# A Mamba and attention layer pair with two expert networks: the second layer's experts dealt out over seven more steps, their sums fetched by plain loads, the flags formed earlier

## The chip, the core and the metric

The kernel runs on one core of one Trainium2 chip. A core has TensorE (PE in the profile; PEld is its weight load), VectorE (DVE), ScalarE (ACT), GpSimd (POOL) and SyncE (SP), which share an on-chip memory, SBUF; TensorE writes to PSUM, and transfers run on sixteen DMA engines. Each engine works through its own instructions in order and waits at semaphores for the others. The metric is the device time of one execution in microseconds, lower is better. Everything is in float32.

## The reference

The input is 8 sequences of 512 tokens with 256 features. Layer 0 adds a two-directional state-space block and a top-1 expert network to it, layer 1 an attention and a top-2 expert network with fixed capacity:

```python
xn = _layernorm(x)
x = x + _L0_attn_ref(xn, ...) + _L0_ffn_ref(xn, ...)
xn = _layernorm(x)
x = x + _L1_attn_ref(xn, ...) + _L1_ffn_ref(xn, ...)
```

The change lies in layer 1. Its attention has 16 heads of width 16; its keys and values come through a latent of width 64, and its scores are scaled, clipped and multiplied by a decay that falls with the distance:

```python
latent_kv = (k + v) @ W_down_kv
scores = clip(einsum('bhqd,bhkd->bhqk', qh, kh) * scale) * decay
out = einsum('bhqk,bhkd->bhqd', softmax(clip(scores)), vh)
return out @ Wo
```

Its expert network sends each of the 4096 tokens to its two best of eight experts. The eighth is a no-op that returns the token weighted; each of the other seven takes its first 512 tokens:

```python
h = relu(einsum('ceh,ehi->cei', inputs, experts_inter))
out = einsum('cei,eih->ceh', h, experts_out) * in_w[..., None]
combined = zeros_like(x_flat).at[used_idx].add(out)
combined = combined + x_flat * (noop_w * noop_mask)[:, None]
```

## The kernel before

**Layer 1 as a loop of steps.** Layer 0 and the routing fill the time until about 1120 us. What the change touches is the loop behind it (`for n in range(N + 2)`, from L1778 on): 128 steps, one for each of 8 batches, 4 groups of 4 heads and 4 blocks of 128 keys, so 16 steps a batch. The order in which instructions are recorded is the order in which each engine works them off. In iteration n stand, in this order: the scores of step n (`scores`: TensorE L1562, then VectorE's product with the decay band and its maxima, L1565, and two small operations, L1570 and L1572); up to six loads of the next batch's q and k rows (`load_some`, L1452, on SP); one move of each chain in `chains`; for step n - 1 ScalarE's exponentials (L1575, L1579) with calls of `soon()` and `fill(1)` between them; the values of step n - 2 (TensorE L1587); the weights of step n - 1 (`weigh`, VectorE L1583), which the values of the next iteration need; then `fill` again.

**Experts between the steps.** `experts()` is a generator over seven experts in two halves of 256 rows each. A half gathers its rows with indirect transfers (L1365, GpSimd), transposes them (L1382), multiplies in eight units with the first weights (L1405, ScalarE's relu L1408) and in eight units with the second (L1418), scales the result (L1422) and adds it into the array `x1` in DRAM with an indirect transfer that accumulates (L1423, GpSimd). Weights are loaded on SP's queue (L1374, L1400). `fill()` draws units while `spent` is below `due()`, a straight line that reaches all of `WORK` at step `LAST = 118`. A unit that stops in the middle of a second product yields True; until its next move `half_done` holds the generator.

**The end of a batch's attention.** `divide(b, g, ...)` is a chain, one move in each iteration. Its group's values go to DRAM (`od`, L1665). For a pair of groups, one iteration later, SP loads them back turned (`oT`, L1675) with the sums of the weights (`sm`, L1676); one iteration after that VectorE takes the minimum into `low` (L1681) and the reciprocals (L1682), SP writes and reads these spread out (`rd` L1683, `rb` L1685), and two iterations later VectorE multiplies (L1688). `oT` is a tile with one buffer for all batches. After the second pair, `finish(b, oT)` comes in front of the list `urgent`: four pieces, each with TensorE's product with the output weights (`fin`, L1522), ScalarE's copy (L1524) and VectorE's sum into the batch's rows in SBUF (`x_sb`, L1526). `soon()` takes one piece of `urgent`, but none while `half_done` is set:

```python
def soon():
    while urgent and not half_done and not late_left:
        if next(urgent[0], "end") != "end":
            return
        urgent.pop(0)
```

**The last batch and the end.** Batch 7 goes another way: its first two groups are turned by TensorE in `first_heads` (L1479 to L1485), also pieces of `urgent`, its last two behind the loop in four `Ending` objects with the parts `out`, `divide`, `back` and `project` (L1498 to L1516). `combine()` adds the experts' sums to `x_sb`: GpSimd issues accumulating loads from `x1` (L1534) for the batches 7 and 0 to 5, then for 6 once its `finish` is through, and then seven stores of whole batches (L1543). Batch 7's rows are stored by `project`, four transfers on SP (L1516). Last, VectorE makes a flag from `peaks`, `vmax` and `low` (L1851 to L1856), TensorE sums it over the partitions (L1858), VectorE casts it (L1860), all five engines read it, and a branch would run an exact version (`exact`) if it were not zero.

Of the kernel before, what the change touches and what calls it, by code (L numbers as in the profile page):

```python
# [17 lines left out]
P = 128  # L18
B, S, DM = 8, 512, 256
NT = B * S  # L20
NTILE = NT // P
TPB = S // P
# [27 lines left out]
KEEP, MOST, LEAST, WIDE = 30.0, 70.0, 1e-8, 1e4  # L50
# [13 lines left out]
def tile_kernel(ctx: ExitStack, tc: tile.TileContext, t, out: bass.AP):  # L64
    nc = tc.nc
    V, A, G, T, Y = nc.vector, nc.scalar, nc.gpsimd, nc.tensor, nc.sync
# [46 lines left out]
    x1 = dram.tile([NT, DM], FP, name="x1", tag="x1")  # L113
# [7 lines left out]
    def rows_of(src, b):  # L121
        return src[b * S : (b + 1) * S, :].rearrange("(c p) d -> p c d", p=P)
# [188 lines left out]
    order = [*range(2, B), 0, 1]  # L311
# [59 lines left out]
    def bank(name, shape, tag="gen"):  # L371
        return mp.tile(shape, FP, name=name, tag=("e", "s")[tag] if isinstance(tag, int) else tag, bufs=2)
# [6 lines left out]
    def rows_in():  # L379
# [29 lines left out]
        for u, b0 in zip(us, order[::2]):  # L409
# [17 lines left out]
            for k, b in enumerate(both):  # L427
# [5 lines left out]
                for o in range(KC):  # L433
# [7 lines left out]
                    else:  # L441
                        A.copy(xTs[b][:, o, :], tp)
            turned.append((both, halves))
        finish(2)
        return xTs

    def step_sizes():

        big = r0b
        v, u, z, z2 = (row(n).rearrange("p (t e) -> p t e", e=2 * NH) for n in ("sp_v", "sp_u", "sp_z", "sp_z2"))  # L450
        V.tensor_tensor(v, proj[:, :, : 2 * NH], bc(dt_bias, 1, D3), ALU.add)
        A.activation(u, v, AF.Abs)
# [12 lines left out]
        V.tensor_scalar(v, v, 0.0, None, ALU.max)  # L465
        V.scalar_tensor_tensor(dt.rearrange(f2), acc.rearrange(f2), 2.0, v.rearrange(f2), ALU.mult, ALU.add)
        V.tensor_scalar(ea, ea, -1.0, None, ALU.mult)
        for d in range(2):
            of = slice(d * NH, (d + 1) * NH)
            V.tensor_tensor(da[:, d], dt[:, :, of], bc(ea[:, of], 1, [P, NTILE, NH]), ALU.mult)  # L470
        yield
# [95 lines left out]
    with ExitStack() as es:  # L567
        p1, p2, psum = m1, m2, mp
# [644 lines left out]
        with tc.manual_schedule(engines=ENGINES):  # L1213

            rows, rest, sizes = itertools.chain(route0(), blocks()), late(), step_sizes()
# [136 lines left out]
    x_sb = res.tile([P, NTILE, DM], FP, name="x_sb", tag="x_sb")  # L1352
    with tc.tile_pool(name="a1", bufs=1) as p1, tc.tile_pool(name="a2", bufs=2) as p2, tc.tile_pool(
        name="ap", bufs=1, space=PSUM
# [100 lines left out]
        def inputs_of(b):  # L1455
            rows, vd = kept[b]
            got = {"q": [], "k": [], "v": p2.tile([P, TPB, VW], FP, name="vt", tag="vt")}
            Y.dma_start(out=got["v"], in_=vd)
            for n in ("q", "k"):
                spread(rows[n], got[n], n)  # L1460
            return got
# [56 lines left out]
        def finish(b, oT):  # L1518
            for c in range(TPB):
                fp = bank("fin", [P, DM])  # L1520
                for j in range(KC):
                    T.matmul(fp, oT[:, j, c * P : (c + 1) * P], w_o[:, j, :], start=(j == 0), stop=(j == KC - 1))  # L1522
                fo = p2.tile([P, DM], FP, name="fo", tag="fo")
                A.copy(fo, fp)  # L1524
                xi = x_sb[:, b * TPB + c, :]
                V.scalar_tensor_tensor(xi, xi, noop[:, b * TPB + c : b * TPB + c + 1], fo, ALU.mult, ALU.add)  # L1526
                yield
            finished.add(b)

        def combine():  # L1530


            def add(b):
                G.dma_start(out=x_sb[:, b * TPB : (b + 1) * TPB, :], in_=rows_of(x1, b), accum_op=ALU.add)  # L1534

            for b in (B - 1, *range(B - 2)):
                add(b)
            yield
            while B - 2 not in finished:
                yield  # L1540
            add(B - 2)
            for b in range(B - 1):
                G.dma_start(out=rows_of(out, b), in_=x_sb[:, b * TPB : (b + 1) * TPB, :])  # L1543

        class Step:
            def __init__(self, b, g, c, inputs):
# [103 lines left out]
        def divide(b, g, op, od, rd, held):  # L1652
# [37 lines left out]
            if g == 3:  # L1690
                urgent.insert(0, finish(b, oT))

        with tc.manual_schedule(engines=ENGINES):
            rows, vd = kept[0]
            got = {"q": [], "k": [], "v": p2.tile([P, TPB, VW], FP, name="vt", tag="vt")}
# [7 lines left out]
            low = p1.tile([P, 32], FP, name="low", tag="low")  # L1703
# [2 lines left out]
            for one in shared:  # L1706
                G.memset(one, 0.0)
            vmax = p1.tile([P, B], FP, name="vmax", tag="vmax")
            finished = set()
            urgent, idle, chains = [], [], []  # L1710
            WORK = NE1 * 2 * (1 + FC + 2 * 4)
            LAST = 118
            spent = 0

            def due():

                return WORK * (n - ready - 2) / (LAST - ready - 2) if ready else 0

            rows, work, ready, e1, number1 = combine(), None, None, None, None
# [57 lines left out]
            tails = []  # L1777
            for n in range(N + 2):  # L1778

                if n < N:  # L1780
                    b, g, c = steps[n]
                    if (g, c) == (2, 0) and b + 1 < B:
                        got = inputs_of(b + 1)
# [32 lines left out]
                if m >= 0:  # L1816
# [4 lines left out]
                    if s.c == TPB - 1:  # L1821
                        if m == N - 1:
                            tails = [Ending(s.b, c, s_op, s.scratch[2]) for c in range(TPB)]
# [8 lines left out]
                    elif spent < due():  # L1832
                        fill()
                follow()
            while urgent:
                soon()
            for _ in rows:
                pass
            for part in ("out", "divide", "back", "project"):
                for one in tails:  # L1840
                    getattr(one, part)()
            while urgent or chains:
                soon()
                for chain in list(chains):
                    if next(chain, "end") == "end":
                        chains.remove(chain)
            for _ in rows:
                pass

            flag = p1.tile([P, 3], FP, name="flag", tag="flag")  # L1850
            V.tensor_reduce(flag[:, 0:1], peaks, AX.X, ALU.max)  # L1851
            V.tensor_reduce(flag[:, 2:3], vmax, AX.X, ALU.max)
            V.tensor_scalar(flag[:, 1:2], flag[:, 2:3], WIDE, None, ALU.is_gt)
            V.scalar_tensor_tensor(flag[:, 0:1], flag[:, 0:1], MOST, flag[:, 1:2], ALU.is_gt, ALU.add)
            V.tensor_reduce(flag[:, 2:3], low, AX.X, ALU.min)
            V.scalar_tensor_tensor(flag[:, 0:1], flag[:, 2:3], LEAST, flag[:, 0:1], ALU.is_lt, ALU.add)  # L1856
            fp = bank("flags", [1, 1])
            T.matmul(fp, flag[:, 0:1], ones[:, 0:1], start=True, stop=True)  # L1858
            bad = p1.tile([1, 1], I32, name="bad", tag="bad")
            V.tensor_copy(bad, fp)  # L1860
            outside = nc.values_load(bad[0:1, 0:1], engines=list(ENGINES), min_val=0, max_val=3 * P)
            with tc.If(outside > 0):
                exact()
# [74 lines left out]
```

## Time and profile before

| what | us |
|---|---|
| median of 3 runs | 1750.51 (1749.23 to 1751.92) |
| the profiled execution | 1758.05 |
| its span, first to last instruction | 1755.9 |
| TensorE busy | 1592.3 |
| VectorE busy | 1193.0 |
| ScalarE busy | 919.0 |
| GpSimd busy | 571.2 |
| first scores of the loop | 1120.3 |
| last values of the loop end | 1740.45 |

The profiled execution took 7.5 more than the median of the timed ones. Times inside it are given from the start of its span. A row of a timeline gives the start, the duration, the engine, the line, the operation, what it writes and reads, how many follow each other, and in brackets the engine's idle time before it and what ended that. SPq rows are transfers that SP issues; they are short, since the transfer itself runs on the DMA engines. A wait for several semaphores is put down to the one that came last in the records, so a transfer named there can be a neighbour of the one that was waited for. TensorE's granted clock is 1.00 at full and 0.50 at half speed.

### The profile page before, as it was taken

How to read it: one execution, taken by the hardware profiler on the slowest of the kernel's cores; microseconds unless marked ns; L12 is line 12 of the kernel's file. 1: busy time of each engine (PE TensorE's matmuls, PEld its weight loads, DVE VectorE, ACT ScalarE, POOL GpSimd, SP SyncE). 2: the span in 40 equal slices, each digit the busy share in tenths (PEclk: the TensorE clock that was granted, in tenths of full speed). 3: DMA queues.
4: the chain of work that ended last, by engine and by line, in shares of the span. 5: the costliest groups of instructions: out<-in, count | busy, mean ns of one | idle time of the engine just before them, and what ended most of it. 6: DMA issues, size and time to landing. Idle time of an engine off the chain costs nothing.

```text
span 1755.9 us, 25860 instructions
## 1 busy us (share of the span) xinstructions
PE 1592.3 (91%) x8736; PEld 952.7 (54%) x8736; DVE 1193.0 (68%) x3111; ACT 919.0 (52%) x2173; POOL 571.2 (33%) x519
## 2 busy tenths in 40 slices
PE   6556799989999999999789889879999999999997
PEld 6323466767677677767455456544444444444432
DVE  6567685575676755865777657476777767767574
ACT  4232345345454454454545533337777777767674
POOL 0041465565565565653522421001111111112030
PEclk9776799999999999999999899769999999999896
DMA  8010355455564464554454624423424333343245
GB/s 299 12 54 0 131 173 186 157 186 177 164 210 158 157 211 150 188 192 134 103 138 139 163 95 115 116 98 86 134 82 116 109 103 113 92 117 118 56 71 148
DMA packets 131789, 230.56 MB, mean 131 GB/s; under 512 B 20093, under 2 KB 93823, under 8 KB 120512
## 3 DMA queue, kind: packets, MB, share of 16 engines
q1 hardware_dynamic: 101952, 119.46, 22.2%
q0 software_dynamic: 28656, 108.69, 20.5%
q8 instruction: 73, 1.20, 0.3%
q10 hardware_dynamic: 1040, 0.66, 0.2%
q14 instruction: 68, 0.56, 0.1%
HBM read 176.23 MB, written 53.05 MB: 131 GB/s over the span
## 4 chain that ended last, share of the span: by engine, by line
PE 42%; DVE 6%; ACT 1%; SPq 1%; issue 1%; DMA 1%; POOL 0%; ACTq 0%; DVEq 0%
PE s_ps L1562 8%; PE o_ps L1587 7%; PE e_hp L1405 6%; PE e_yp L1418 6%; PE fin L1522 2%; PE qp L265 1%; PE pj L933 1%; PE tab L230 1%; PE op L1078 1%; DVE s L1565 1%; PE pp L762 1%; PE seg L1121 1%; PE sp L1189 1%; PE kp L274 1%; PE yd L1159 1%
## 5 line engine op out<-in xcount | busy, mean ns | idle before, releaser
L1565 DVE CUSTOM_DVE_ANT_0 s<-s_ps,band 128x512 f32<-128x512 f32 x512 | 323.0, 687 | 152.8 <-PE s_ps L1562 152.7
L1579 ACT ACTIVATE s<-s,ng 128x512 f32<-128x512 f32 x512 | 334.0, 710 | 0.0
L933 PE MATMUL pj<-xT,w_w_in 128*128 128x512 f32 x384 | 199.9, 647 | 10.1 <-DVE cv L946 6.2
L1423 POOL DMA_INDIRECT x<-e_yo,number x28 | 45.0, 1606 | 431.9 <-ACT e_yo L1422 230.0
L1562 PE MATMUL s_ps<-qT,kT 16*128 16x512 f32 x1024 | 167.7, 694 | 4.4 <-DMA kT<-kd 4.4
L946 DVE SCALAR_TENSOR_TENSOR cv<-pj,w_conv_w,cv 128x511 f32<-128x511 f32 (+2 forms) x192 | 143.2, 747 | 22.4 <-ACT cv L942 17.9
L1587 PE MATMUL o_ps<-s,wv 128*32 128x512 f32 x1024 | 150.0, 659 | 5.5 <-DVE wv L1583 4.7
L1105 POOL TENSOR_TENSOR au<-da,half 128x512 f32<-128x512 f32 x64 | 76.4, 1193 | 235.6 <-PE seg L1121 163.1
L639 PEld LDWEIGHTS h_ps<-xdT,w 128*128 128x128 f32 x1152 | 139.1, 194 | 20.8 <-issue 20.0
L639 PE MATMUL h_ps<-xdT,w 128*128 128x128 f32 x1152 | 142.1, 277 | 2.2 <-DMA w<-in_w_dram,w_idx 2.2
L663 PE MATMUL y_ps<-w,hT 128*128 128x256 f32 x576 | 138.7, 385 | 0.0
L1418 PE MATMUL e_yp<-e_w,e_hT 128*128 128x256 f32 x448 | 125.8, 405 | 0.0
L1418 PEld LDWEIGHTS e_yp<-e_w,e_hT 128*128 128x128 f32 x448 | 77.5, 191 | 88.2 <-issue 65.5
L663 PEld LDWEIGHTS y_ps<-w,hT 128*128 128x128 f32 x576 | 108.3, 193 | 30.0 <-issue 16.1
L1405 PE MATMUL e_hp<-e_xdT,e_w 128*128 128x256 f32 x448 | 123.3, 400 | 0.0
L1405 PEld LDWEIGHTS e_hp<-e_xdT,e_w 128*128 128x128 f32 x448 | 78.6, 190 | 76.8 <-ACT e_hT L1408 37.7
L933 PEld LDWEIGHTS pj<-xT,w_w_in 128*128 128x128 f32 x384 | 70.4, 201 | 91.6 <-issue 81.9
L1134 ACT ACTIVATE mt<-seg,mid 64x64 f32<-64x64 f32 x512 | 109.4, 309 | 0.8
L1168 DVE TENSOR_TENSOR yT<-yT,yd 128x512 f32<-128x512 f32 (+1 forms) x64 | 43.8, 684 | 96.5 <-PE yd L1159 96.5
L950 ACT ACTIVATE th<-cv 128x512 f32<-128x512 f32 x64 | 40.3, 630 | 118.5 <-DVE cv L946 109.0
L942 ACT ACTIVATE cv<-pj,w_conv_b,w_conv_w 128x512 f32<-128x512 f32 x64 | 49.8, 778 | 89.9 <-PE pj L933 85.8
L1153 DVE TENSOR_TENSOR mt<-mt,cbm 128x1024 f32<-128x1024 f32 x64 | 94.1, 1471 | 1.2 <-ACT mt L1134 1.1
(339 smaller groups left out, 2794.6 us busy)
## 6 DMA issues: line engine op xcount, KB each, us to landing
ex<-exd SPq DMA_DIRECT2D x96, 128.0 KB
fr<-fdd SPq DMA_DIRECT2D x64, 128.0 KB
od<-os SPq DMA_DIRECT2D x28, 256.0 KB
e_w<-in_ei_dram SPq DMA_DIRECT2D x7, 1024.0 KB
e_w<-in_eo_dram SPq DMA_DIRECT2D x7, 1024.0 KB
vd<-vt SPq DMA_DIRECT2D x16, 272.0 KB
vt<-vd SPq DMA_DIRECT2D x8, 544.0 KB
u<-in_u_dram SPq DMA_DIRECT2D x8, 512.0 KB
```

The costliest lines, as they stand in the source:

```text
L639: T.matmul(hp[:, i, :], w1[:, k * FF + f * P : k * FF + (f + 1) * P], xdT[:, k * P : (k + 1) * P], start=(k == 0), stop=(k == KC - 1),)
L663: T.matmul(yp, hT[f // 4][:, f % 4, :], w2[:, f * DM : (f + 1) * DM], start=(f == 0), stop=(f == FC - 1),)
L933: T.matmul(pj, w_in[:, k, o * P : (o + 1) * P], self.xT[:, k, :], start=(k == 0), stop=(k == KC - 1))
L946: V.scalar_tensor_tensor(cv[:, s:], pj[:, : S - s], conv_w[:, q, 3 - s : 4 - s], cv[:, s:], ALU.mult, ALU.add)
L1134: A.activation(mt[lo, over, h], seg[lo, over, h], AF.Exp, bias=mid[lo, self.i, h : h + 1])
L1153: V.tensor_tensor(self.mt, self.mt, bc(self.cbm, 1, H3), ALU.mult)
L1405: T.matmul(hp, w1[:, k, f * P : (f + 1) * P], xdT[:, k, :], start=(k == 0), stop=(k == KC - 1))
L1418: T.matmul(yp, hT[:, f, c * P : (c + 1) * P], w2[:, f, :], start=(f == 0), stop=(f == FC - 1))
L1562: T.matmul(sp[i], self.k[r, cols], self.q[r, :], start=True, stop=True)
L1565: V.tensor_tensor_reduce(out=self.p[i], in0=sp[i], in1=band[:, at : at + S], scale=1.0, scalar=KEEP, op0=ALU.mult, op1=ALU.max, accum_out= ...
L1579: A.activation(self.p[i], self.p[i], AF.Exp, bias=self.ng[:, i : i + 1])
L1587: T.matmul(op[32 * i : 32 * i + 32, :], self.wv[:, i, :], self.p[i], start=(self.c == 0), stop=(self.c == TPB - 1),)
```

## The change

Four things change. `LAST` goes from 118 to 125, so that `due()` spreads the experts' units over seven more steps. `combine()` no longer accumulates by transfers: when the units are spent, the expert pools are closed, eight tiles `xa` take their place, SP loads `x1` into them with plain transfers, GpSimd adds the batches 7 and 0 to 4 and stores 0 to 4, and VectorE adds 5 and 6 after the loop, which GpSimd stores. The calls that emptied `urgent` and `rows` ahead of the last tiles' parts go. The flag's operations are recorded between these parts, with a fourth column for the minimum and the cast on ScalarE, and TensorE's sum stands ahead of `project`.

```diff
         def combine():
-            def add(b):
-                G.dma_start(out=x_sb[:, b * TPB : (b + 1) * TPB, :], in_=rows_of(x1, b), accum_op=ALU.add)
-
-            for b in (B - 1, *range(B - 2)):
-                add(b)
-            yield
-            while B - 2 not in finished:
+            es.close()
+            p3 = es.enter_context(tc.tile_pool(name="f3", bufs=1, side="right"))
+            order = (B - 1, *range(B - 1))
+            got = {}
+            for b in order:
+                got[b] = p3.tile([P, TPB, DM], FP, name="xa", tag=f"xa{b}")
+                Y.dma_start(out=got[b], in_=rows_of(x1, b))
+
+            def add(engine, b):
+                own = x_sb[:, b * TPB : (b + 1) * TPB, :]
+                engine.tensor_tensor(own, own, got[b], ALU.add)
+                if b < B - 1:
+                    G.dma_start(out=rows_of(out, b), in_=own)
+
+            for b in order[:-2]:
+                add(G, b)
+            while not closing:
                 yield
-            add(B - 2)
-            for b in range(B - 1):
-                G.dma_start(out=rows_of(out, b), in_=x_sb[:, b * TPB : (b + 1) * TPB, :])
+            for b in order[-2:]:
+                add(V, b)
+                yield
...
-            LAST = 118
+            LAST = 125
...
-            while urgent:
-                soon()
-            for _ in rows:
-                pass
-            for part in ("out", "divide", "back", "project"):
-                for one in tails:
-                    getattr(one, part)()
             while urgent or chains:
                 soon()
                 for chain in list(chains):
                     if next(chain, "end") == "end":
                         chains.remove(chain)
-            for _ in rows:
-                pass
-
-            flag = p1.tile([P, 3], FP, name="flag", tag="flag")
+            closing = True
+            flag = p1.tile([P, 4], FP, name="flag", tag="flag")
             V.tensor_reduce(flag[:, 0:1], peaks, AX.X, ALU.max)
             V.tensor_reduce(flag[:, 2:3], vmax, AX.X, ALU.max)
             V.tensor_scalar(flag[:, 1:2], flag[:, 2:3], WIDE, None, ALU.is_gt)
             V.scalar_tensor_tensor(flag[:, 0:1], flag[:, 0:1], MOST, flag[:, 1:2], ALU.is_gt, ALU.add)
-            V.tensor_reduce(flag[:, 2:3], low, AX.X, ALU.min)
-            V.scalar_tensor_tensor(flag[:, 0:1], flag[:, 2:3], LEAST, flag[:, 0:1], ALU.is_lt, ALU.add)
+            for part in ("out", "divide"):
+                for one in tails:
+                    getattr(one, part)()
+            V.tensor_reduce(flag[:, 3:4], low, AX.X, ALU.min)
+            V.scalar_tensor_tensor(flag[:, 0:1], flag[:, 3:4], LEAST, flag[:, 0:1], ALU.is_lt, ALU.add)
+            for one in tails:
+                one.back()
+            next(rows, None)
             fp = bank("flags", [1, 1])
             T.matmul(fp, flag[:, 0:1], ones[:, 0:1], start=True, stop=True)
             bad = p1.tile([1, 1], I32, name="bad", tag="bad")
-            V.tensor_copy(bad, fp)
+            A.copy(bad, fp)
+            for one in tails:
+                one.project()
+            for _ in rows:
+                pass
```

More of the change, by code (lines that the diff above doesn't have):

```diff
@@ L1527, in finish @@
                 yield
-            finished.add(b)
         def combine():
-            def add(b):
-                G.dma_start(out=x_sb[:, b * TPB : (b + 1) * TPB, :], in_=rows_of(x1, b), accum_op=ALU.add)
-            for b in (B - 1, *range(B - 2)):
-                add(b)
-            yield
-            while B - 2 not in finished:
+            es.close()
[13 more added lines that the diff above has]
+            while not closing:
                 yield
-            add(B - 2)
-            for b in range(B - 1):
-                G.dma_start(out=rows_of(out, b), in_=x_sb[:, b * TPB : (b + 1) * TPB, :])
+            for b in order[-2:]:
+                add(V, b)
+                yield
         class Step:
@@ L1708, in tile_kernel @@
             vmax = p1.tile([P, B], FP, name="vmax", tag="vmax")
-            finished = set()
+            closing = False
             urgent, idle, chains = [], [], []
             WORK = NE1 * 2 * (1 + FC + 2 * 4)
-            LAST = 118
+            LAST = 125
             spent = 0
```

## The prediction

> **What bounds the kernel now.** I read the page first, then the stretches of the last stage by window, then the chain of waits and the engines' timelines around the two places where TensorE stops, last the end.
>
> ```profile
> span 1755.9 us, 25860 instructions
> PE 1592.3 (91%) x8736; PEld 952.7 (54%) x8736; DVE 1193.0 (68%) x3111; ACT 919.0 (52%) x2173; POOL 571.2 (33%) x519
> ```
>
> ```profile
> 1600.00:1637.50 37.50, 37.50 (x212) 18.17 (x211) 27.08 (x98) 27.24 (x57) 5.35 (x4) 1.00 0.40 123
> 1637.50:1644.50 7.00, 5.04 (x28) 2.23 (x27) 2.37 (x11) 4.26 (x8) 0.00 (x0) 0.97 0.25 69
> 1644.50:1655.00 10.50, 10.01 (x36) 3.73 (x36) 6.67 (x25) 4.59 (x10) 1.63 (x1) 0.53 0.34 66
> 1655.00:1695.00 40.00, 40.00 (x230) 17.76 (x230) 29.48 (x108) 29.08 (x60) 3.60 (x3) 1.00 0.15 34
> 1708.00:1740.00 32.00, 28.76 (x118) 7.46 (x114) 19.28 (x76) 18.71 (x38) 6.76 (x9) 0.52 0.89 208
> ```
>
> Above the page, below it stretches of the last stage. Columns: stretch, length, busy time of PE, PEld, DVE, ACT, POOL, then the granted clock. While expert work is dealt out, PE is busy all the time at clock 1.00: the 128 attention steps go at PE's pace. Behind step 118 PE runs at 0.52. In between lies one hole, 1637.5 to 1655, with the clock at 0.53 after it.
>
> The price of a step is read from the chain of waits: scores 1.07, expert unit 1.06, values 0.99, expert unit 1.06, together 4.19; a further unit behind another adds 1.92 - 1.06 = 0.86.
>
> ```profile
> 1656.24 1.06 PE e_yp L1418 x4
> 1657.30 0.99 PE o_ps L1587 x8
> 1658.30 1.06 PE e_yp L1418 x4
> 1659.36 1.07 PE s_ps L1562 x8
> ...
> 1666.67 1.92 PE e_hp L1405 x8
> ```
>
> The hole, as timelines of SP's queue, VectorE and PE:
>
> ```profile
> 1629.53 0.34 SPq L1665 DMA_DIRECT2D od<-os  x1
> 1637.52 0.55 SPq L1675 DMA_DIRECT2D oT<-od  x1
> ...
> 1639.09 0.16 DVE L1572 TENSOR_SCALAR w<-peaks 128x4 f32<-128x4 f32 x1
> 1643.82 0.19 DVE L1681 TENSOR_TENSOR low<-low,sm 128x32 f32<-128x32 f32 x1 [4.57 <-DMA kT<-kd]
> ...
> 1636.36 1.13 PE L1522 MATMUL fin<-w_w_o,oT 128*128 128x256 f32 x4
> 1641.41 1.13 PE L1418 MATMUL e_yp<-e_w,e_hT 128*128 128x256 f32 x4
> 1644.99 1.94 PE L1587 MATMUL o_ps<-s,wv 128*32 128x512 f32 x8 [2.45 <-DVE wv L1583]
> ```
>
> `oT` has one buffer. SP cannot load batch 6's `oT` until PE has done batch 5's last `fin`: that ends at 1637.49, the load goes at 1637.52. Behind it stands the load of `sm`; VectorE, in order, waits for it in `low` (L1681) until 1643.82, 6.3 after `fin`; behind `low` stands `wv` (L1583), behind `wv` PE's values at 1644.99, 7.5 after `fin`. Count a batch's steps from its first: `low` stands in step 11 and holds the weights for the values that PE issues in step 12. In the built order the last `fin` of batches 0 to 5 stands in steps 10, 10, 10, 10, 11, 11 of the batch behind. At 10 the trace shows no hole; at 11 both batches have one: 2.23 of PE's idle time at 1570 (clock kept), and 2.45 at 1645, with the clock lost for some 10 us.
>
> **The change, part by part** (against the profiled run: span 1755.9, 1758.05 around it, 7.5 above the median of the timed runs; I carry the difference over to the median).
>
> *Experts to step 125.* 224 units in steps 8 to 118 become 224 in steps 8 to 125. The built order has 222 units done by the end of step 117 before and 208 after: 14 x 0.86 = 12.0 earlier. Steps 118 to 125: four with a `fin` and two units 5.05 each, one with two transposes 4.5, three at 4.19, together 37.3; before, scores of 118 to scores of 126 took 1727.2 - 1689.5 = 37.7. Sum: -12.4. Filling the cold steps with units costs them nothing, since without them they run at half clock.
>
> *What the new pace does to `fin`.* `soon()` does nothing while a y-part of an expert is half done, so another phase of the units moves the `fin`s. In the changed order the last one of batches 0 to 5 stands in steps 11, 12, 12, 12, 10, 9. At 12, PE reaches the values held up right behind it: `fin`, one unit (0.86), then values that may start 7.5 after `fin` (8.2 in the earlier hole): a hole of 6.6 to 7.4, I take 7.0. To that comes the clock: around the hole at 1645 two steps (scores to scores, 1640.34, 1648.86, 1655.1) took 8.52 and 6.24 where their parts sum to 4.19 and 3.72, so 6.85 more, of which 2.5 is the wait and 4.3 the half clock. The earlier hole of 2.2 cost 2.3. A hole of 7.0 is nearer to the one that lost its clock, being longer than both: 7.0 + 4.3 = 11.3 each, three times, 33.9; bounds 6.6 without and 7.4 + 5.0 where half of some 10 us at half clock is lost. Batch 1's hole (step 11) is of the old kind: 2.3 to 6.85, taken as 5.0. The two old holes go: -9.2. Sum: +29.7. `sm`, `rd`, `rb` and the next batch's kT loads move with SP; kT is needed four steps on and stays hidden.
>
> The row on the clock is 0.53 for 1644.5 to 1655 though PE was busy for 10.01 of the 10.50. The Trainium skill ("TensorE: Matmul & The Clock Gate", section "What's actually happening") has the array warm again after one busy window of about 3.4 us, at half rate until then. By that a lost clock would cost at most 1.7 in place of 4.3, and the sum would fall by some 9; this trace's row disagrees, and I keep the row.
>
> *First heads later.* Step 126 takes transposes and column work that stood in step 122: 5.0 there, 4.29 for a bare step at half clock: +1. From the scores of 127 to the last values 8.9 before; after, two more transposes but a warmer clock: 0, between -1 and +2.
>
> *Plain loads, adds, stores.* Now this:
>
> ```profile
> 1694.52 1.55 POOL L1423 DMA_INDIRECT x<-e_yo,number  x1 [6.83 <-ACT w L1575]
> 1698.90 10.53 POOL L1534 DMA_DIRECT2D x_sb<-x  x8 [2.83 <-DVE wv L1583]
> ...
> 1724.66 0.75 POOL L1543 DMA_DIRECT2D out_dram<-x_sb  x1 [1.91 <-DMA x_sb<-x]
> ...
> 1747.40 0.42 DVE L1515 TENSOR_TENSOR x_sb<-x_sb,finq 128x256 f32<-128x256 f32 x1 [0.44 <-PE finq L1514]
> ...
> 1749.44 0.15 DVE L1860 CAST bad<-flags 1x1 int32<-1x1 f32 x1 [0.28 <-PE flags L1858]
> ```
>
> The accumulating loads and the stores ended under the last steps; after step 118 they had 50 us. Now they have step 126 to the end. Let O be the end of the last values (1740.45 before). The scores of step 126 start at O - 14.1 (5.2 + 8.9). The last scatter lands 4.6 after the unit before them (1693.7 to 1698.3), the first 512 KB load needs some 2.9 (two such loads issued at 1604.9 were in at 1610.5, so 2.8 each): POOL starts adding at O - 6.6. No row has a 128x1024 add on POOL; 128x512 takes 1042 ns at the median in L1148 and 1260 in L1183, whose operands are alike: 2.1 to 2.5, taken 2.25. Six adds 13.5, seven stores issued at 0.75 to 0.96, 6.2: POOL is through at O + 13.1. VectorE meanwhile: `finq` adds end at O + 7.4 before; the low flag (0.34) and one 128x1024 add (1219 ns at the median in L1153) stand ahead of them, one behind: O + 10. POOL is later and sets the end. From the last `bad` read (1749.7) to the end there were 6.2; before, O + 15.4, now O + 19.3: +3.9, between +2.5 (adds of 2.1) and +6. The flag chain that leaves VectorE (1.6) lies before POOL's end and brings nothing.
>
> A pair of VectorE and POOL operations with two inputs in SBUF is the place where the Trainium skill ("SBUF — State Buffer", section "Who interferes with whom") speaks against the change: one waits for the whole other. L1153's longest, 6398 ns against a median of 1219, agrees with it. By the rule VectorE's two adds wait up to 2.25 each, O + 14.5; by the row's median O + 10; the end would move by 1.4 at most.
>
> **Sum:** -12.4 + 29.7 + 1 + 3.9 = +22.2: 1778 as a span, 1750.5 + 22.2 = **1772.7** as a median.
>
> **The rivals.**
> (a) *The late `fin` is hidden and no hole appears*: then -12.4 - 9.2 + 1 + 3.9 = -16.7, 1733.8. It decides if `sm` lands before VectorE is through with step 11, that is if the last `fin` is at least 6.3 ahead of `low`. For it: four batches show no hole now. Against: those have it in step 10, none in 12. Chance 0.09.
> (b) *Holes, but the clock holds*, as at 1570: 3 x 7.0 + 2.9 = 23.9 in place of 38.9: +7.2, 1757.7. Against: the longer of the two holes lost it. Chance 0.2.
> (c) *POOL becomes the bound by more*: adds twice as long as the row (L1105 has a longest of 2106 against 1042): 6 x 2.25 = +13.5, 1786. For it: VectorE works beside it; against: its scores read one operand from PSUM, and 1191 is the mean in L1020. Chance 0.1.
> The forecast itself has 0.61.
>
> **How the numbers follow.** The measurement tells about 0.2%, 3.5 us, from no change. Faster: (a) 0.09 and the low end of (b) 0.01. Same: 0.04 out of (b), where the holes are 6.6 and the tail +2.5. Slower: the rest, 0.86. The range runs from (b) less 3 to the forecast with holes of 12.5 (3 x 1.2) and batch 1 and the tail at their upper ends (2 + 2), with 5 more for (c): 1755 to 1785. Left out: (a) and most of (c).
>
> **What would show it.** `fin` before `oT` in SP's queue, and VectorE idle some 10 before `low` in batches 2, 3, 4 (steps 43, 59, 75), some 5 in batch 1; PE idle 6.6 to 7.4 at each of the three with the clock near 0.5 behind; no hole in batches 5 and 6. Units until step 125 at clock 1.00. At the end POOL adding after VectorE's `finq` adds. I am wrong if PE is busy without a break from step 10 to 125, or if POOL's adds end before the last values.

## The result and the profile after

The changed kernel takes 1773.99 us (median; 1771.48 to 1779.96), the kernel before 1749.87 (1739.02 to 1751.92) on the same chip: a ratio of 1.0137, with a 95% interval of 1.0100 to 1.0175. It is slower, by about as much as forecast (1772.7). Not every term of that sum was right, though, and two errors offset each other in part.

The profiled executions differ by less than the medians: spans of 1755.9 before and 1769.7 after, +13.8 against +24.1, because the one of before lay 8.2 above its median and the one of after 2.5 below its own. Executions of one kernel scatter here by some 0.5 to 0.8% to either side. The terms below are read from the two traces, the verdicts from the timed runs.

From the page of the kernel after, the span, the busy times, and the group of the values (out and in tiles, count, busy time, mean ns, then TensorE's idle time ahead of it and what ended most of that):

```profile
span 1769.7 us, 25893 instructions
PE 1585.9 (90%) x8736; PEld 948.5 (54%) x8736; DVE 1196.8 (68%) x3112; ACT 920.8 (52%) x2174; POOL 578.8 (33%) x517
...
L1593 PE MATMUL o_ps<-s,wv 128*32 128x512 f32 x1024 | 147.0, 649 | 21.1 <-DVE wv L1589 21.1
```

TensorE works 6.4 us less than before, and yet the span is 13.8 longer. It stands 21.1 us in front of the values, waiting for `wv`; the same group had 4.7 before.

The stage by window, around the hole in step 44 (stretch, length, busy time of PE, PEld, DVE, ACT, POOL, granted clock, share of the DMA engines, GB/s):

```profile
1300.00:1347.70 47.70, 47.70 (x276) 21.79 (x268) 34.98 (x126) 36.31 (x75) 9.17 (x7) 1.00 0.37 105
1347.70:1354.20 6.50, 3.08 (x17) 1.75 (x16) 0.00 (x0) 3.67 (x8) 0.00 (x0) 1.00 0.20 55
1354.20:1361.00 6.80, 3.26 (x11) 1.38 (x12) 4.20 (x16) 0.00 (x0) 0.00 (x0) 0.50 0.59 174
1361.00:1400.00 39.00, 39.00 (x228) 16.80 (x227) 28.75 (x104) 30.89 (x64) 5.36 (x4) 1.00 0.33 100
```

TensorE is busy without a break before and behind. Between 1347.7 and 1361.0 it stands for 6.95, and the clock is at 0.50 for 6.8, the first half of which falls into the standstill. VectorE does nothing at all in the first of the two stretches.

The same hole in the timelines of SP's queue, VectorE and TensorE (start, duration, engine, line, operation, tiles; in brackets the idle time before and what ended it):

```profile
1337.38 0.34 SPq L1671 DMA_DIRECT2D od<-os  x1
...
1339.62 1.03 SPq L1452 DMA_DIRECT2D kT<-kd  x2
1349.95 0.54 SPq L1681 DMA_DIRECT2D oT<-od  x1
1350.54 0.52 SPq L1682 DMA_DIRECT2D sm<-od  x1
...
1346.47 0.17 DVE L1578 TENSOR_SCALAR w<-peaks 128x4 f32<-128x4 f32 x1
1356.66 0.19 DVE L1687 TENSOR_TENSOR low<-low,sm 128x32 f32<-128x32 f32 x1 [10.03 <-DMA sm<-od]
...
1357.46 0.23 DVE L1589 TENSOR_TENSOR wv<-vt,w 128x68 f32<-128x68 f32 x1
...
1348.79 1.13 PE L1522 MATMUL fin<-w_w_o,oT 128*128 128x256 f32 x4
1349.76 1.03 PE L1405 MATMUL e_hp<-e_xdT,e_w 128*128 128x256 f32 x4
1357.74 1.94 PE L1593 MATMUL o_ps<-s,wv 128*32 128x512 f32 x8 [6.95 <-DVE wv L1589]
```

The heads of the pair were sent to DRAM at 1337, and from 1340.7 on nothing stands ahead of the load in SP's queue (with two `oT`, below, SP issues it right behind the same kT loads). Here it goes at 1349.95, right behind the old batch's last `fin` (1348.79 + 1.13). From there everything follows in a row: `sm` is in at 1356.6, VectorE has been idle for 10.03 in front of `low`, `wv` comes behind it, and TensorE's values 7.8 after `fin`, with one unit between. Steps 60 and 76 have the same picture with 6.08 and 6.15 of TensorE's idle time, step 28 the smaller one with 1.92.

The end of the kernel after, timelines of SP's queue, GpSimd, VectorE and TensorE (last values end at 1747.0):

```profile
1736.17 8.48 SPq L1537 DMA_DIRECT2D xa<-x  x8
...
1741.38 4.67 POOL L1541 TENSOR_TENSOR x_sb<-x_sb,xa 128x1024 f32<-128x1024 f32 x2 [7.67 <-DMA xa<-x]
...
1757.65 2.36 POOL L1541 TENSOR_TENSOR x_sb<-x_sb,xa 128x1024 f32<-128x1024 f32 x1
1760.32 2.26 POOL L1543 DMA_DIRECT2D out_dram<-x_sb  x3 [0.30 <-POOL x_sb L1541]
...
1750.23 2.90 DVE L1856 SCALAR_TENSOR_TENSOR flag<-flag 128x1 f32<-128x1 f32 x1
...
1758.75 0.42 DVE L1515 TENSOR_TENSOR x_sb<-x_sb,finq 128x256 f32<-128x256 f32 x1 [0.44 <-PE finq L1514]
...
1753.18 0.19 PE L1861 MATMUL flags<-ones,flag 128*1 128x1 f32 x2 [2.63 <-DVE flag L1856]
```

GpSimd adds from 1741.4 to 1760.0 and issues its last store until 1762.6, after VectorE's last `finq` sum (1759.2): GpSimd and its stores end the kernel, 22.7 behind the last values, against 15.4 before. A flag operation on one element per partition takes 2.90 in place of 0.16; TensorE waits 2.63 for it.

To set the traces side by side I counted for each step from 8 on what it takes beyond the parts of its work (the 4.19 with two units and the 0.86 of a third in the prediction):

| | before | after | difference |
|---|---|---|---|
| scores of step 8 start | 1187.2 | 1183.4 | -3.8 |
| steps 8 to 125 by their parts | 526.4 | 513.6 | -12.8 |
| beyond the parts (the holes) | 13.6 | 34.3 | +20.7 |
| scores of step 126 to the end of the last values | 13.25 | 15.7 | +2.45 |
| from there to the end | 15.45 | 22.7 | +7.25 |
| span | 1755.9 | 1769.7 | +13.8 |

(For before, the row of parts has 492.9 up to step 118 and 33.5 for the stretch from the scores of 119 to those of 126.) Of the 34.3, steps 28 and 29 hold 5.2, step 44 8.6, step 60 8.0 and step 76 8.0; of the 13.6, steps 92, 108 and 109 hold 9.15. Step 8 has some 3 in every run.

### The profile page after: what moved, and what is told of

Read it like the earlier page. It is cut to its first block, busy times and chain, and to the rows that moved or that the text cites. A ratio compares the mean times of both kernels' runs of the same rounds, so it can differ in the third digit from the quotient of the medians.

```text
span 1769.7 us, 25893 instructions
## 1 busy us (share of the span) xinstructions
PE 1585.9 (90%) x8736; PEld 948.5 (54%) x8736; DVE 1196.8 (68%) x3112; ACT 920.8 (52%) x2174; POOL 578.8 (33%) x517
## 3 DMA queue, kind: packets, MB, share of 16 engines
q1 hardware_dynamic: 106176, 123.66, 22.3%
## 4 chain that ended last, share of the span: by engine, by line
PE 43%; DVE 5%; DMA 1%; ACT 1%; SPq 1%; issue 1%; POOL 0%; DVEq 0%; ACTq 0%; POOLq 0%
PE s_ps L1568 8%; PE o_ps L1593 8%; PE e_yp L1418 7%; PE e_hp L1405 6%; PE pj L933 2%; PE fin L1522 2%; PE qp L265 1%; PE tab L230 1%; PE op L1078 1%; PE pp L762 1%; DMA sm<-od 1%; PE yd L1159 1%; PE seg L1121 1%; PE sp L1189 1%; PE kp L274 1%
## 5 line engine op out<-in xcount | busy, mean ns | idle before, releaser
L1593 PE MATMUL o_ps<-s,wv 128*32 128x512 f32 x1024 | 147.0, 649 | 21.1 <-DVE wv L1589 21.1
L1568 PE MATMUL s_ps<-qT,kT 16*128 16x512 f32 x1024 | 160.2, 678 | 4.6 <-DMA kT<-kd 4.6
L639 PEld LDWEIGHTS h_ps<-xdT,w 128*128 128x128 f32 x1152 | 137.7, 192 | 21.2 <-issue 20.4
L1405 PE MATMUL e_hp<-e_xdT,e_w 128*128 128x256 f32 x448 | 128.4, 411 | 0.0
L663 PEld LDWEIGHTS y_ps<-w,hT 128*128 128x128 f32 x576 | 106.8, 190 | 29.4 <-issue 16.1
```

The source lines that it names most:

```text
L639: T.matmul(hp[:, i, :], w1[:, k * FF + f * P : k * FF + (f + 1) * P], xdT[:, k * P : (k + 1) * P], start=(k == 0), stop=(k == KC - 1),)
L663: T.matmul(yp, hT[f // 4][:, f % 4, :], w2[:, f * DM : (f + 1) * DM], start=(f == 0), stop=(f == FC - 1),)
L1405: T.matmul(hp, w1[:, k, f * P : (f + 1) * P], xdT[:, k, :], start=(k == 0), stop=(k == KC - 1))
L1568: T.matmul(sp[i], self.k[r, cols], self.q[r, :], start=True, stop=True)
L1593: T.matmul(op[32 * i : 32 * i + 32, :], self.wv[:, i, :], self.p[i], start=(self.c == 0), stop=(self.c == TPB - 1),)
```

## The experiments

**Is the hole made by `oT`'s one buffer, and by the new pace alone?** My theory was that SP's `oT` load waits for the late `fin`. A rival was that the traffic of the units or the order of VectorE's work makes the holes in any case, another that the change of the end has a part in them. Four kernels tell these apart: a second buffer for `oT` in the kernel after and in the kernel before, `LAST` alone at 125 in the kernel before, and `LAST` back at 118 in the kernel after.

```diff
-                    held.append(p1.tile([P, KC, S], FP, name="oT", tag="oT"))
+                    held.append(p1.tile([P, KC, S], FP, name="oT", tag="oT", bufs=2))
```

(the same at the other two places that make an `oT`)

> The changed kernel with two buffers for oT, nothing else. Theory (the late fin holds SP's load of oT, that holds VectorE at low, that holds PE's values): the holes of steps 28, 44, 60, 76, together 31 us over the parts' sum in the changed kernel's trace, go, down to 1 or 2; time 1774 - 30 = 1744, 1739 to 1750. Rival A (the holes come from the experts' pace itself, by their weights' transfers on SP's queue): two buffers change nothing, 1774. Rival B (the change is slow by its end: GpSimd's adds and stores behind the last values): 1774 too, with the holes gone but the time not.

Measured: 1743.33 (1731.87 to 1748.68) against 1756.84 for the kernel before, a ratio of 0.9921 (0.9892 to 0.9951). The span of its profile is 1746.1. The time beyond the parts falls from 34.3 to 4.1, as expected; what is left lies mostly in step 8, and no step from 9 on has a hole. The end stays, at 23.1 behind the last values. Its timelines at the same batch:

```profile
1342.29 0.54 SPq L1681 DMA_DIRECT2D oT<-od  x1
1342.88 0.52 SPq L1682 DMA_DIRECT2D sm<-od  x1
...
1350.15 0.19 DVE L1687 TENSOR_TENSOR low<-low,sm 128x32 f32<-128x32 f32 x1 [1.78 <-DMA sm<-od]
...
1350.53 1.13 PE L1522 MATMUL fin<-w_w_o,oT 128*128 128x256 f32 x4
...
1352.46 1.06 PE L1593 MATMUL o_ps<-s,wv 128*32 128x512 f32 x8
```

The last `fin` is still late, at 1350.53, but SP has issued the loads 8.2 before it, `low` waits 1.78, and the values run on at full clock.

> The kernel before with two buffers for oT, nothing else. Theory: its two holes, 9.2 us with the half clock behind them, go: 1750 - 9 = 1741, 1737 to 1746. Rivals A and B: no difference, 1750.

Measured: 1751.90, a ratio of 0.9975 (0.9948 to 1.0002). Its profile has no hole either (4.2 beyond the parts in place of 13.6). In the traces that is worth 9.4; the timed runs show about 4.4, with an interval that just reaches no change. I had expected 9. So the two holes of the kernel before are real, but either they cost less in its usual execution than in the profiled one, or a second buffer costs something elsewhere; the runs don't settle which. With the second buffer on both sides the change is worth about 0.5% by the timed runs (0.9921 / 0.9975); the two profiled spans, 1746.1 and 1745.2, do not show it.

```diff
-            LAST = 118
+            LAST = 125
```

> The kernel before with the experts dealt out to step 125, and nothing else of the change. Theory: the order's fins stand as in the changed kernel, so the same four holes (31 us in place of 11, +20), the loop's units earlier (-12.5), and the accumulating loads and stores, 21 and 10 us of transfers in the trace of before, now start behind step 126 and end some 38 after its scores in place of 28.7: +9 to +11. 1750 + 20 - 12.5 + 10 = 1767, 1760 to 1774. Rival B (the end of the change alone is slow): no holes' cost, 1750 - 12.5 + 10 = 1748.

Measured: 1786.38, a ratio of 1.0176 (1.0120 to 1.0232). The kernel before with the new pace alone shows the holes of the kernel after, step by step: 5.4 in steps 28 and 29, 8.3, 8.4 and 7.9 in steps 44, 60 and 76, together 34.6 beyond the parts. So the pace makes them, without any part of the new end. Its timelines, TensorE in step 44 and GpSimd at the end:

```profile
1361.01 1.94 PE L1587 MATMUL o_ps<-s,wv 128*32 128x512 f32 x8 [6.60 <-DVE wv L1583]
...
1736.06 1.55 POOL L1423 DMA_INDIRECT x<-e_yo,number  x1 [6.83 <-ACT w L1575]
1740.56 10.53 POOL L1534 DMA_DIRECT2D x_sb<-x  x8 [2.96 <-DMA x<-e_yo,number]
...
1769.62 0.75 POOL L1543 DMA_DIRECT2D out_dram<-x_sb  x1 [4.26 <-DMA x_sb<-x]
```

The accumulating transfers, which were hidden at `LAST` 118, come out into the open: the end is 29.6 behind the last values. That is why it is slower than the 1% I had expected. Against it, the plain loads and adds of the change are worth 29.6 - 22.7 = 6.9 at this pace.

> The changed kernel with the experts dealt out to step 118 as before: plain loads, adds and the flags' new places stay. Theory: fins and holes as in the kernel before, and the adds lie under steps 120 to 127; from the last values to the end 15.4 less the flag chain's 1.6 plus one add of 1.2 and a store's issue: 1750, 1745 to 1755. Rival B: the adds cost where they stand, 1757 or more.

Measured: 1764.11 (1749.29 to 1774.47), a ratio of 1.0034 (1.0001 to 1.0067). I had expected no difference; the rival, that the adds cost where they stand, fits better. The end is as short as before (16.1), what lies beyond the parts is close to before (16.3 for 13.6), but the stretch from the scores of 119 to those of 126 takes 40.7 in place of 33.5. GpSimd, VectorE and TensorE in that stretch:

```profile
1720.76 2.36 POOL L1541 TENSOR_TENSOR x_sb<-x_sb,xa 128x1024 f32<-128x1024 f32 x1
1723.42 0.77 POOL L1543 DMA_DIRECT2D out_dram<-x_sb  x1 [0.30 <-POOL x_sb L1541]
1724.21 2.37 POOL L1541 TENSOR_TENSOR x_sb<-x_sb,xa 128x1024 f32<-128x1024 f32 x1
...
1720.59 2.56 DVE L1576 TENSOR_SCALAR ng<-peaks 128x4 f32<-128x4 f32 x1
...
1723.65 3.02 DVE L1589 TENSOR_TENSOR wv<-vt,w 128x68 f32<-128x68 f32 x1
...
1712.83 1.94 PE L1593 MATMUL o_ps<-s,wv 128*32 128x512 f32 x8 [3.33 <-DVE wv L1589]
...
1723.88 0.45 PE L1484 MATMUL tb<-ident,oq 128*128 128x128 f32 x1 [3.17 <-DVE oq L1470]
```

`ng` (0.17 elsewhere) ends at 1723.15 and GpSimd's add at 1723.12; `wv` (0.22 elsewhere) ends at 1726.67 and the next add at 1726.58. VectorE's small operations last until GpSimd's sum is through, and TensorE waits 3.33, 1.21 and 3.17 in these steps. `wv` is recorded from 1723.65 on, 0.56 ahead of its sum, while GpSimd still issues a store; the store is not what holds it, since under a store with no sum behind it `wv` took 0.21 (at 1725.90 in the last kernel below, with `LAST` at 122). The next kernel tests the sums as a cause: the same sums, in about the same steps, on VectorE.

```diff
-            for b in order[:-2]:
-                add(G, b)
+            for _ in range(4):
+                yield
+            for b in order[:-2]:
+                add(V, b)
+                for _ in range(3):
+                    yield
```

> In the kernel after with LAST at 118 the scores of step 119 to those of step 126 take 40.7 us, against 33.5 in the kernel before, and TensorE waits 3.33 and 1.21 and 3.17 there behind VectorE. Here the same six sums are added by VectorE in place of GpSimd, one behind the weights of each of the steps 119 to 124. My theory: an add on GpSimd (2.36 us) holds off VectorE's operations with two inputs in SBUF and the small ones of four columns until it ends, since 1.94, 2.40, 1.02, 2.56 and 3.02 us of such operations each end together with an add. Without adds on GpSimd no weights (wv) and no ng take over 0.3 in these steps; VectorE has some 4.2 us of work in a step with its own add (1.22), about what TensorE has at half clock, so the stretch from 119 to 126 falls to 33.5 to 35.5. The end stays at 15.5 to 16.5 behind the last values. The time falls from 1.0034 of before to 0.999 to 1.001. Rival: the eight plain loads, or the lost clock, hold TensorE up whichever engine adds; then the stretch stays at 39 or more and the time at 1.003 or above.

Measured: 1753.79 against 1754.97, a ratio of 1.0000 (0.9971 to 1.0029). The stretch is back to 34.5, as expected, and the end is 15.1 behind the last values (15.5 to 16.5 expected). The durations of `wv`, least, median and longest in ns, with GpSimd's sums (first fence) and with VectorE's (second):

```profile
L1589 DVE TENSOR_TENSOR wv<-vt,w x128: 165/223/3025, 1130.3 to 1748.9; 128x68 f32<-128x68 f32 x128
```

```profile
L1593 DVE TENSOR_TENSOR wv<-vt,w x128: 166/223/244, 1128.8 to 1739.1; 128x68 f32<-128x68 f32 x128
```

The longest falls from 3025 to 244. The eight plain loads are the same in both, and the half clock lies over both stretches, so it is GpSimd's sums that held VectorE off. The rival falls.

**Does it have to be the buffer?** If the cause is that the load stands behind a late `fin`, an earlier `fin` must do as well, with one buffer. So `soon()` may work while a second product is half done:

```diff
-                while urgent and not half_done and not late_left:
+                while urgent and not late_left:
```

> The changed kernel with one buffer for oT, but soon() no longer waits while a y-part is half done; the order then has the last fin in step 9 for every batch. Theory (the hole is the lateness of fin, and fin is late for half_done): no holes, steps 8 to 125 within 5 us of their parts' sum as with two buffers, against 34 in the changed kernel; time as with two buffers, 0.99 of the kernel before, 0.985 to 0.996. Rival (the second buffer helped in another way, by its place in memory or by letting oT load early): holes stay, 1.014.

Measured: 1744.32, a ratio of 0.9935 (0.9903 to 0.9967) to the kernel before (1753.38 here). The last `fin` stands in step 9 in every batch, and 6.7 remains beyond the parts; of the holes, 1.31 us of idle time is left in step 44, at full clock. In step 44 SP issues the `oT` load at 1343.68 with one buffer. What VectorE waited for in front of `low` (us, times), first in the kernel after, then in this one:

```profile
  DMA sm<-od: 26.4, 7
  DMA kT<-kd: 8.6, 1
```

```profile
  DMA sm<-od: 10.7, 8
```

Two edits that share nothing but that `fin` no longer stands before the load both take the long holes away. The rivals fall.

**What sets the end?** Starting from the kernel with two `oT`, the flag's two operations with two inputs in SBUF become operations with one, and TensorE's sum runs over three columns:

```diff
-            V.scalar_tensor_tensor(flag[:, 0:1], flag[:, 0:1], MOST, flag[:, 1:2], ALU.is_gt, ALU.add)
+            V.tensor_scalar(flag[:, 0:1], flag[:, 0:1], MOST, None, ALU.is_gt)
...
-            V.scalar_tensor_tensor(flag[:, 0:1], flag[:, 3:4], LEAST, flag[:, 0:1], ALU.is_lt, ALU.add)
+            V.tensor_scalar(flag[:, 2:3], flag[:, 3:4], LEAST, None, ALU.is_lt)
...
-            T.matmul(fp, flag[:, 0:1], ones[:, 0:1], start=True, stop=True)
+            for k in range(3):
+                T.matmul(fp, flag[:, k : k + 1], ones[:, 0:1], start=(k == 0), stop=(k == 2))
```

> The changed kernel with two oT buffers, and the flag's two operations with two SBUF inputs replaced by ones with one input, TensorE summing three columns. Theory on the end: a VectorE operation with two SBUF inputs waits for a GpSimd add (1.37 and 2.90 us for operations of 0.16); with one input it does not, so these take 0.16 and TensorE's flags wait 2.6 less; but GpSimd's adds and stores are through last and set the end: last values to end 23.1 becomes 22 to 23. Rival (the flags set the end): 20 to 20.5.

Measured: 1740.87 in a single execution, span 1739.2, and 22.9 from the last values to the end against 23.1 without the edit. VectorE's timeline:

```profile
1719.54 0.15 DVE L1856 TENSOR_SCALAR flag<-flag 128x1 f32<-128x1 f32 x1
1720.36 4.00 DVE L1541 TENSOR_TENSOR x_sb<-x_sb,xa 128x1024 f32<-128x1024 f32 x1 [0.67 <-DMA xa<-x]
1724.29 1.40 DVE L1515 TENSOR_TENSOR x_sb<-x_sb,finq 128x256 f32<-128x256 f32 x4
```

The flag takes 0.15 now, under one of GpSimd's sums, and TensorE's flag sum no longer waits for it. But with two `oT` there was less to take away than the 2.90 I had in mind from the kernel after. There the same operation and the 128x1024 sum behind it had taken this:

```profile
1726.19 0.52 DVE L1856 SCALAR_TENSOR_TENSOR flag<-flag 128x1 f32<-128x1 f32 x1
1727.56 3.74 DVE L1541 TENSOR_TENSOR x_sb<-x_sb,xa 128x1024 f32<-128x1024 f32 x1 [0.84 <-DMA xa<-x]
```

So this edit by itself hardly tests the rival. The three traces together speak against it: TensorE's flag sum starts 6.2 behind the last values in the kernel after, 3.8 with two `oT` and 3.5 here, and the end comes 22.7, 23.1 and 22.9 behind them. An earlier flag did not bring an earlier end.

Then VectorE takes four of the eight sums from GpSimd (`order[:-4]` and `order[-4:]`, two of them ahead of TensorE's flag sum), and in a second kernel `LAST` is 122 as well:

> As two_oT_flags, and GpSimd adds four batches, VectorE four: two ahead of the flags' sum on TensorE, two at the end. Theory: GpSimd is through 2 x 2.36 + its pauses, some 5, earlier, VectorE some 2.4 later: last values to end 23 becomes 18 to 19.5, time 4 less than with two buffers alone: 0.990 of the kernel before, 0.985 to 0.993. Rival (the end waits for stores' landing, not for the adds): no difference to two_oT_flags.

> As two_oT_flags_vector with the experts dealt out to step 122. Theory: six more units before step 122 cost 6 x 0.86 = 5.2 earlier and three steps without units save up to 3 x 4.19 - 3 x 4.3 = 0, so the last values come some 5 later at most, less where bare steps run at full clock; loads and adds start three steps, 13, earlier against the values, so last values to end falls from 19 to 15 to 16. Sum 0 to +2: 0.990 to 0.992. Rival (the end's chain hardly depends on when the experts end): +4 to +5.

Measured: 1743.72, ratio 0.9957 (0.9926 to 0.9988), and 1748.66, ratio 0.9961 (0.9934 to 0.9988), which can't be told apart. In the first GpSimd is through 13.6 behind the last values in place of 16.4, and yet the end is only 0.6 earlier (22.3), where I had expected 18 to 19.5. My theory, that GpSimd's issue of the last store sets the end, fails there. The DMA engines show a part of why: from GpSimd's last store on they run full (columns as above; the last two are the share of the DMA engines and GB/s).

```profile
1737.30:1740.00 2.70, 0.00 (x0) 0.00 (x0) 0.00 (x0) 0.00 (x0) 0.03 (x1) 0.50 1.00 321
1740.00:1742.50 2.50, 0.00 (x0) 0.00 (x0) 0.00 (x0) 0.00 (x0) 0.00 (x0) 0.50 0.71 250
```

The kernel with six sums on GpSimd sends its last stores at the same rate (309 and 344 GB/s from 1732 to 1736), so a part of the earlier issue is waited off in the queues: the last packet of GpSimd's stores ends 18.6 behind the last values in place of 20.4. The other part is SyncE. The rows below are its four stores of batch 7 and the DRAIN instructions at the end of GpSimd's and SyncE's programs (count, shortest, median and longest in ns, first and last start), first with six sums on GpSimd, then with four:

```profile
1724.72 2.21 SPq L1516 DMA_DIRECT2D out_dram<-x_sb  x4
...
L1933 POOLq DRAIN  x3: 46/113/4980, 1733.2 to 1738.7; - x3
L1933 SPq DRAIN  x3: 7/7/13, 1737.7 to 1738.4; - x3
```

```profile
1733.05 3.59 SPq L1516 DMA_DIRECT2D out_dram<-x_sb  x4
...
L1933 POOLq DRAIN  x3: 46/112/5782, 1738.3 to 1745.7; - x3
L1933 SPq DRAIN  x3: 7/7/13, 1745.1 to 1745.4; - x3
```

GpSimd's long DRAIN ends 21.8 behind the last values in the first and 20.4 in the second; SyncE's first comes at 21.4 in both. So in the second SyncE, which did not get earlier, is the last one through. Its stores took 3.59 to issue in place of 2.21; whether the full queues make the difference was not tested.

With `LAST` at 122 the end is 4.5 shorter (17.8, where 15 to 16 was expected) and the last values are 9 later, of which 1.7 lie ahead of step 8 (some 5 at most was expected); step 60 has 2.1 beyond its parts again, steps 123 to 125 have 6.9 of idle time and half clock, and a `wv` under GpSimd's sums takes 3.11.

The lowest ratio with an interval is that of the changed kernel with two buffers for `oT` alone: 0.9921 of the kernel before. Its interval overlaps those of the other three without long holes (0.9935, 0.9957, 0.9961), so they can't be ranked; no run with an interval shows a gain from the further edits. Against the changed kernel the ratio of the two ratios is 0.9921 / 1.0137 = 0.979.

## Why the prediction was right, and where it was not

**The order of terms held.** The likeliest case, late `fin`, three long holes and a lost clock, is what happened, and the two kernels without the late load show that it is the cause of the loss: without it the change is 0.8% (two buffers) or 0.65% (earlier `fin`) faster than before.

*Experts to step 125: -12.4.* The parts give -12.8. Outside the holes the clock is 1.00 until the last unit, and units filled the cold steps as said.

*The late `fin`: +29.7.* The traces give +20.7. The place and the chain are as described: steps 44, 60 and 76 with the large hole, batch 1 with the small one (5.2 where 5.0 was put), no hole in batches 5 and 6, VectorE idle for 10.0, 9.2 and 8.6 in front of `low`, `fin` to values 7.8. The wait of 7.0 measured 6.95, 6.08 and 6.15. The term that failed is "A hole of 7.0 is nearer to the one that lost its clock": from that I took 4.3 of half clock for each hole. The three steps hold 8.6, 8.0 and 8.0 beyond their parts; less the wait, the clock cost 1.6, 1.9 and 1.9. Of the 9.0 that the term was too large, the clock makes some 7.5 and the shorter waits the rest. The half clock lasts 6.8 us each time, and TensorE stands for the first 3.5, 2.3 and 2.6 of it. At step 44 it works from 1357.7 and has the full clock from 1361.0: 3.3 us of work, half of which is lost.

This is what I decided against in the prediction. The Trainium skill ("TensorE: Matmul & The Clock Gate", section "What's actually happening") has the array warm again after one busy window of about 3.4 us; by the term I drew from it, at most 1.7 a hole and some 9 less in the sum. The three long holes agree with it to 0.2. The row that I preferred, 10.2 us at half clock with TensorE busy, is not wrong either: with `LAST` at 118 the loss at the same place lasts 17.1 in the kernel with GpSimd's sums and 10.2 in the one with VectorE's, some 50 us before either begins its sums. But it stands behind short holes, and it does not carry over to long ones. Behind a short hole all or nearly all of the period lies under work: in step 28 of the kernel after (1.92 of idle time) 6.8 us, which cost 3.3. Behind a long one a third to a half of the 6.8 lies in the standstill. The periods of 6.8, 10.2 and 17.1 are two, three and five times the page's window; why busy windows were not enough behind the short holes stays open.

Whether a short hole loses the clock at all can be read from the traces, though no run moves a hole to test it. The recorded clock changes on a raster of 3.41 us. In every short hole of these runs while units are dealt out, the clock fell where one interval of the raster held 1.54 us of idle time or more (1.92 in step 28 of the kernel after; 1.54 of the 2.45 at 1642.5 in the kernel before). It held where an interval had 1.40 or less: the 2.23 at 1568.2 in the kernel before was cut into 0.83 and 1.40, and the 2.00 in step 60 with `LAST` at 122 into 0.84 and 1.16.

*The two old holes: -9.2.* In the traces, right (9.15). In the timed runs the buffer that removes them brings 4.4 with an interval of 0 to 9, so the term may have been too large for the usual execution.

*First heads later: +1.* +2.45. The clock fell in step 127 and stood at 0.67 for the stretch, and one `wv` of step 127 took 0.97 under GpSimd's first sum.

*The end: +3.9.* +7.25. The claim that GpSimd ends after VectorE held, and so did its price (2.36 a sum for 2.25). What I left out were the 0.30 that GpSimd stands before each store that follows a sum, and that it starts 1.0 later (the first sum came 5.2 after the first load's issue, where 2.9 stood in the working): it is through at 15.6 behind the last values instead of 13.1. The rest is the landing: 7.1 from the last issue to the end in place of the 6.2, which I had taken from the flag's read in the kernel before, where no store was under way. That stores on full queues set the end was not in the working.

*VectorE and GpSimd: at most 1.4.* For the end of the kernel after this was about right, since the 1.2 and 2.7 that the flag operations lost lie before GpSimd's end. As a judgement on the change it was too narrow, since I looked for the price in the two large sums alone. With `LAST` at 118 the same sums stand under the steps, and there they cost 40.7 - 34.5 = 6.2. The Trainium skill ("SBUF — State Buffer", section "Who interferes with whom") says of GpSimd and a VectorE operation in a two-port mode: "Whoever issues first gets the shared pair for the whole instruction; the other **fully blocks** (not throttle)." On blocking the runs agree to 0.1: VectorE's 3.02 and 2.56 end with GpSimd's sums. On who comes first they do not show it: both operations are recorded as starting ahead of their sum, by 0.56 and 0.17. The section counts VectorE operations with two SBUF inputs among those that contend with GpSimd's reads, which `wv` and the flag's old form are, and `tensor_scalar` where it runs in a two-port mode. That would fit `ng`, on four columns, being held and the flag's new form, on one, not; no run here tests that mode by itself.

**Why the total came out so near.** The holes were 9.0 too dear, the end and the heads 4.8 too cheap, and the rest is the profiled executions: their difference is 13.8, of which -3.8 lies ahead of the loop's step 8, and the medians differ by 10.3 more. The forecast added terms to the profiled execution and carried the result over to the median; that the errors and this scatter nearly cancel is luck, and the range, not the digit, is what the working supported.

**The rivals.** (a) No hole: fell. (b) Holes with the clock held: fell as stated, since the clock was lost at each, but its size was the nearer one (23.9 for all four, measured 29.8; the forecast's was 38.9). (c) GpSimd twice as slow: fell, 2.36 against 4.5.

## What to carry to other kernels

Before slowing down or speeding up one stream of work in a fixed order, look for the tile with one buffer that two streams share, and count who stands behind its load in the queue: here a load waited for a product that now came up to two steps later, a minimum of 0.19 us for the next load in that queue, and TensorE for both. The change's gain was there all along, hidden under a wait that a second buffer, or an earlier product, removed. And when work moves to GpSimd, price what it does to every small VectorE operation beside it, not only its own time.

## What the runs showed of the hardware

- GpSimd adds two 128x1024 tiles in 2.36 us, VectorE in 1.22. While GpSimd does, VectorE's 128x68 product takes up to 3.11 (0.22 alone), a 128x4 `tensor_scalar` up to 2.56 (0.17), a 128x1 `scalar_tensor_tensor` 2.90 (0.16); a 128x1 `tensor_scalar` 0.15, the scores' product that reads PSUM 0.69 as ever.
- Standstills of TensorE of 6 to 7 us cost 1.6 to 1.9 of half clock each, one of 1.92 us cost 3.3, one of 2.45 us some 4.3: these short ones cost more, since nearly all of the slow period lies under work. Others of 2.23 and 2.00 us, cut by the raster of 3.41 us, cost none.
- While GpSimd's last 512 KB stores leave, the DMA engines move some 310 to 340 GB/s until they run out; with `LAST` at 122 or 125 the kernels with the new end were through 6.4 to 8.7 us after the last was issued.
- Eight plain 512 KB loads were issued by SP in 8.5 us, the first sum began 5.2 after the first issue.
